# The last feed-forward layer's first batch: rows turned by VectorE and DMA in place of TensorE, their low parts by GpSimd

## The chip, the cores and the metric

The kernel runs on one core of a Trainium2 chip. The metric is the device time of one execution in microseconds (us); before the change the median of three runs is 2222.36 us (2220.96 to 2223.24). The engines are named as in the profile: PE is TensorE, DVE is VectorE, ACT is ScalarE, POOL is GpSimd, and SP is the engine whose queue issues most DMAs.

## The reference, cut to what matters

The input is a batch of 8 sequences of 512 rows and 512 columns, float32. Two layers follow each other, and each of their four parts ends in a layer norm over the rows:

```python
x = layernorm(x + attention0(x))        # 16 heads of 32, causal
x = layernorm(x + experts(x))           # 8 experts, the two best of each row
# layer 1's attention: 8 heads of 64 over 2 groups of keys, no mask
h = norm_scale * x / (rms(x) + EPS) * split_scale
out = softmax(q @ k.T / 8) @ v          # q, k, v are products of h
x = layernorm(x + out @ Wo.T)
# layer 1's feed-forward part, integer weights
g = silu(x @ ((wq_gate - 128) * s_gate).T)
u = x @ ((wq_up - 128) * s_up).T
x = layernorm((g * u) @ ((wq_down - 128) * s_down).T)
```

The change lies where the third part (layer 1's attention) ends and the fourth (the "last FFN") begins.

## The kernel before, in words

**The last FFN** (`IntegerFfn`) works on one batch of 512 rows after another. Its matmuls need the batch's rows turned: columns of `x` on the 128 partitions, rows along the free axis, as four tiles of 128 x 512. Each turned tile is kept as two: `x_high`, the value rounded to the format that TensorE multiplies fast (fp32r), and `x_low`, the rest, so that two fast products stand for one float32 product. ACT writes the high part and DVE subtracts it from the turned tile for the low part.

There are two ways to turn the rows. `split` (L1102 to L1110), used for batch 0 alone, has TensorE transpose sixteen blocks of 128 x 128, four to a PSUM tile (L1108); ACT copies the tile to `x_high` (L1109) and DVE takes `x_low` (L1110). `blocks` and `parts` (L1083 to L1099), used for batches 1 to 7 inside the FFN, have DVE transpose 32 x 32 blocks (L88, four instructions of 128 x 512), send the room to DRAM with four DMAs (L93) and fetch it with a fifth (L96), which puts the blocks where they belong; then ACT casts (L1098) and DVE subtracts (L1099) from SBUF. This way leaves the rows in another order along the free axis, and `hidden` (L1135) undoes it where it reads the products and writes their halves: for `b` above 0 the access patterns of L1148's tile and of the two halves (L1153, L1154) go through `Turn.by_tile`.

Batch 0 is turned while layer 1's attention does its last batch, number 7.

**Layer 1's attention** (`Attention1`) does a batch in eight rounds, 0 to 7. A batch has four queries, `g` = 0 to 3, of two heads each, and each query has four blocks of 128 keys, `kt` = 0 to 3. A round does two blocks of one query, so query `g` takes rounds 2g and 2g + 1. The order inside a round is written out by hand in `batches` and holds on PE, DVE, ACT and POOL; SP's DMAs are ordered by a scheduler. A round issues, in this order:

1. `score`: four matmuls into two PSUM tiles `sc` (L1702), and two exponentials of 128 x 1024 on ACT (L1705) into two of four buffers `p`;
2. `add` for the blocks of the round before: DVE sums the `p` tiles into `total` (L1713), one instruction in an odd round, two in an even one;
3. the pieces that `plan` lists for the round: a query's projection (L1607, eight matmul records, and ACT's copy L1609), the output projection of the batch before (L1670, then DVE's L1676, L1684, L1685);
4. `product` for the blocks of the round before: `av` (L1724);
5. where that completes a query, so in even rounds, `normalise` (L1729): two matmuls `rs` of `total` with ones (L1732), ACT's copy with a sum (`watch_sums`, L995), DVE's reciprocal (L1735) and product (L1742), and POOL's `watch_inverses` (L998), which adds the reciprocal to a running total.

So `rs` on PE waits for the DVE's sums of the query, and the exponentials of a round wait for buffers of `p` that `add` and `product` of two rounds before have to have read. `total`, `r_inv` and the query's tile `hT` have one buffer each.

In batch 7 `plan` puts query 1 in round 0, query 2 in round 1, query 3 in round 5, output projections in rounds 2, 3, 4 and 7, and `split` of one of the four tiles in each of rounds 0, 2, 4 and 6.

Of the kernel before, what the change touches and what calls it, by code (L numbers as in the profile page):

```python
# [9 lines left out]
F32 = mybir.dt.float32  # L10
# [4 lines left out]
ALU = mybir.AluOpType  # L15
# [3 lines left out]
P = 128  # L19
NB = 8  # L20
S = 512
D = 512
NT = S // P
ND = D // P
# [33 lines left out]
def in_order(tc, *engines):  # L58


    return tc.manual_schedule(engines={mybir.EngineType.PE, *engines})
# [11 lines left out]
class Turn:  # L73
# [11 lines left out]
    def blocks(self, room, t, x):  # L85

        out = room.rearrange("p (j t c) -> p j t c", t=self.n, c=32)[:, :, t, :]
        self.nc.vector.transpose(out, x.rearrange("p (j c) -> p j c", c=32))  # L88
# [328 lines left out]
class Router:  # L417
# [70 lines left out]
    def logits(self, x1T, ps):  # L488

        for c in range(ND):  # L490
            self.nc.tensor.matmul(ps[32 * c : 32 * (c + 1), :], lhsT=self.wr[:, c, :], rhs=x1T[:, c, :],
                                  start=True, stop=True)

    def choose(self, b, parts, ps):

        nc, small = self.nc, self.small
# [300 lines left out]
class Tiles:  # L797
# [83 lines left out]
    def weights(self, i, c):  # L881
        at = self.ats[i]
        if i < N_FIXED:
            return self.w[:, at + c * 512 : at + (c + 1) * 512]
        return self.w[:, bass.ds(at + c * 512, 512)]
# [180 lines left out]
class IntegerFfn:  # L1066
# [13 lines left out]
        self.halves[b] = [pool.tile([P, ND, S], F32R, tag=f"rows{i}", name=f"x3_{part}")  # L1080
                          for i, part in enumerate(("high", "low"))]

    def blocks(self, b, t):  # L1083

        if t == 0:
            self.room(b)
            self.turned = self.raw.tile([P, ND * S], F32, tag="turned", name="turned")
        turn = self.turns[b % 2]
        turn.blocks(self.turned, t, self.env.xs[b][:, t, :])
        if t == NT - 1:  # L1090
            turn.out(self.turned)
            turn.back(self.turned)

    def parts(self, b, c):

        high, low = (half[:, c, :] for half in self.halves[b])
        x = self.turned[:, ts(c, S)]
        self.nc.scalar.copy(high, x)  # L1098
        self.nc.vector.tensor_tensor(low, x, high.bitcast(F32), ALU.subtract)  # L1099

    def split(self, b, c, ps):

        nc = self.nc
        if c == 0:
            self.room(b)
        high, low = self.halves[b]
        for t in range(NT):
            nc.tensor.transpose(ps[:, ts(t, P)], self.env.xs[b][:, t, ts(c, P)], self.env.ident)  # L1108
        nc.scalar.copy(high[:, c, :], ps)  # L1109
        nc.vector.tensor_tensor(low[:, c, :], ps, high[:, c, :].bitcast(F32), ALU.subtract)  # L1110

    def run(self, held_out, last_norm):
        tc, nc, weights = self.env.tc, self.nc, self.weights
# [21 lines left out]
    def hidden(self, b, c, held):  # L1135

        nc, vec, work, weights = self.nc, self.env.vec, self.work, self.weights
        g = self.p_gu.tile([P, S], F32, tag="g", name="ps_g1")
        u = self.p_gu.tile([P, S], F32, tag="u", name="ps_u1")
        for ps, w in ((g, weights(2 * c)), (u, weights(2 * c + 1))):  # L1140
            for dc in range(ND):
                for i, x in enumerate(self.halves[b]):
                    nc.tensor.matmul(ps, lhsT=w[:, ts(dc, P)], rhs=x[:, dc, :],  # L1143
                                     start=(dc, i) == (0, 0), stop=(dc, i) == (ND - 1, 1))
        sg = work.tile([P, S], F32, tag="sg", name="sg1", bufs=2)
        nc.scalar.activation(sg, g, AF.Silu, scale=vec[:, V_SG + c : V_SG + c + 1])
        hT = work.tile([P, S], F32, tag="hT", name="hT2", bufs=2)
        nc.vector.scalar_tensor_tensor(hT, u, vec[:, V_SU + c : V_SU + c + 1], sg, ALU.mult, ALU.mult)  # L1148
        high, low = (self.late.tile([P, S], F32R, tag=f"h{i}", name="h_late") if held else
                     work.tile([P, S], F32R, tag=f"h{i}", name="h_half", bufs=2) for i in range(2))  # L1150

        hT, *halves = [self.turns[0].by_tile(a, back) if b else a for a, back in ((hT, True), (high, False), (low, False))]
        nc.scalar.copy(halves[0], hT)  # L1153
        nc.vector.tensor_tensor(halves[1], hT, halves[0].bitcast(F32), ALU.subtract)  # L1154
        return high, low
# [381 lines left out]
class Attention1:  # L1537
# [94 lines left out]
        for part in (self.w_qkv[:, c, :], self.w_qkv[:, ND : ND + 2, ts(c, P)]):  # L1632
            self.nc.scalar.mul(part, part, self.nss[:, c : c + 1])

    def run(self, weights, split):

        with ExitStack() as phase:
            self.work = work = phase.enter_context(self.env.tc.tile_pool(name="c_work", bufs=1, reuse_waits="tile"))
            p_sc = phase.enter_context(self.env.tc.tile_pool(name="c_sc", bufs=2, space=PSUM, reuse_waits="tile"))
            p_av = phase.enter_context(self.env.tc.tile_pool(name="c_av", bufs=2, space=PSUM, reuse_waits="tile"))  # L1640
            with in_order(self.env.tc, mybir.EngineType.DVE, mybir.EngineType.Activation, mybir.EngineType.Pool):
                return self.batches(work, p_sc, p_av, weights, split)

    def batches(self, work, p_sc, p_av, weights, split):
        env, nc, guard, state, HD = self.env, self.nc, self.guard, self.state, self.HD
        xs = env.xs
        scale = 1.0 / math.sqrt(HD)
# [14 lines left out]
        def project(b, t):  # L1662
            ps = self.mm([P, D], "ps_o1")
            project_groups(b, t, ps, range(ND))
            residual(b, t, ps)
            statistics(b, t)
# [24 lines left out]
        def norm(b):  # L1691
            st = state.pop(b)
            for t in range(NT):
                x = xs[b][:, t, :]
                nc.vector.tensor_scalar(x, x, st["mv"][:, t, 0:1], st["rstd"][:, t : t + 1], ALU.subtract, ALU.mult)
# [49 lines left out]
        def plan(b):  # L1745


            todo = [[] for _ in range(ND * NT // 2)]
            here = pieces.pop(b)
            first, final = b == 0, b == NB - 1  # L1750
            if first:
                pieces[1] = self.prepare(1)
                todo[0] += [lambda t=t: pieces[1]["fetch"](t) for t in range(NT)]
            then = pieces.get(b + 1)
            if b:
                for t, i in enumerate((2, 3, 4, 7) if final else (2, 3, 4, 5)):
                    todo[i].append(lambda t=t: project(b - 1, t))
                if not final:
                    todo[6].append(lambda: norm(b - 1))
            for g, i in zip((1, 2, 3), (1, 3, 5) if first else (0, 1, 5) if final else (0, 1, 3)):  # L1760
                todo[i].append(lambda g=g: here["query"](g))
            if final:
                for c, i in enumerate((0, 2, 4, 6)):
                    todo[i].append(lambda c=c: split(0, c, self.mm([P, S], "ps_xT")))
            else:
                if first:

                    for t, i in ((2, 1), (3, 2)):
                        todo[i].append(lambda t=t: then["sum"](t))
                        todo[i + 2].append(lambda t=t: then["stat"](t))  # L1770
                for t, i in ((0, 1), (1, 2)) if first else ((0, 0), (1, 1), (2, 1), (3, 2)):
                    todo[i].append(lambda t=t: then["add"](t))
                if first:
                    todo[4].append(then["deviations"])

                    todo[5].insert(0, then["norm"])
                    todo[6] += [lambda c=c: then["turn"](c) for c in range(ND)]
                else:
                    todo[2].append(then["deviations"])
                    todo[3].append(then["norm"])  # L1780
                    todo[3] += [lambda t=t: then["blocks"](t) for t in range(NT)]
                todo[6].append(then["key"])
                todo[7] += [then["value"], lambda: then["query"](0)]
                if b + 2 < NB:
                    after = pieces[b + 2] = self.prepare(b + 2)
                    todo[7] += [lambda t=t: after["fetch"](t) for t in range(NT)]
            for i in (7,) if first else (1, 7) if final else (5, 7):
                todo[i] += [weights.convert, lambda: weights.load(work, 2, weights.FIRST)]
            return todo

        last = []
        for b in range(NB):
            for i, thunks in enumerate(plan(b)):
                units = [(b, u // NT, u % NT) for u in (2 * i, 2 * i + 1)]
                ps = [score(*unit) for unit in units]
# [12 lines left out]
        b = NB - 1  # L1808
# [16 lines left out]
def usual_pass(tc, ins, held_out):  # L1825
    nc = tc.nc
    with ExitStack() as ctx:
# [4 lines left out]
        with tc.tile_pool(name="a_mm", bufs=2, space=PSUM) as p_mm, ExitStack() as attn1_ctx:  # L1832
            with tc.tile_pool(name="routes", bufs=1, side="right") as routes, \
# [11 lines left out]
                attention = Attention1(env, guard, router, rows, own, p_mm, dram)  # L1845
# [15 lines left out]
            weights = IntegerWeights(env, guard)  # L1861
            weights.open(ctx.enter_context(tc.tile_pool(name="c_weights", bufs=1, side="right")), weights.FIRST)
            ffn = IntegerFfn(env, guard, weights, rows, dram)
            last_norm = attention.run(weights, ffn.split)
        ffn.run(held_out, last_norm)


# [236 lines left out]
def _layout(a):  # L2104
# [18 lines left out]
    def hidden(w):  # L2123
        return w.reshape(NHID, P, ND, P).transpose(0, 3, 2, 1).reshape(NHID, P, D)

    gate_up_q = np.stack([hidden(a["L1_ffn_wq_gate"]), hidden(a["L1_ffn_wq_up"])], axis=1).reshape(2 * NHID, P, D)

    def rows(n):
# [43 lines left out]
```

## Time and profile before

| What | us |
|---|---|
| median of the runs | 2222.36 |
| the profiled execution | 2228.55 |
| its span, first to last instruction | 2226.8 |
| PE busy | 2191.9 (98%) |
| DVE busy | 1273.7 (57%) |
| ACT busy | 632.0 (28%) |
| POOL busy | 487.6 (22%) |
| batch 7's rounds in the span | 1643 to 1702 |
| first matmul of the last FFN | 1722.78 |

Times within an execution are counted from the span's start. The profiled execution is 6.2 us above the median of the runs. "Busy" counts instructions of an engine; an engine that is idle shows the wait and who released it.

### The profile page before, as it was taken

The page shows a single profiled execution, that of the slowest core. Times are in us where ns is not written, and L with a number is a line of the kernel's source. Part 1 is how long each engine was busy: PE and PEld are TensorE (multiplying, and loading weights), DVE is VectorE, ACT ScalarE, POOL GpSimd, SP SyncE. Part 2 cuts the span into 40 slices and gives each one's busy share as a digit, 9 for nine tenths or more (in the row PEclk, how much of TensorE's full clock was granted, in tenths as well). Part 3 has the DMA queues.
Part 4 walks back from the last instruction along what each step waited for, and adds up shares of the span by engine and source line. Part 5 has one row for each costly group of instructions (what it writes and reads, how often), then busy time and mean ns, then how long its engine had stood idle before and what let it go on. Part 6 is the DMA issues. An engine that isn't in the chain of part 4 may idle for free. (4 is left out here: it accounts for less than half of the span.)

```text
span 2226.8 us, 23678 instructions
## 1 busy us (share of the span) xinstructions
PE 2191.9 (98%) x9006; PEld 1116.6 (50%) x9006; DVE 1273.7 (57%) x2032; ACT 632.0 (28%) x917; POOL 487.6 (22%) x489
## 2 busy tenths in 40 slices
PE   9999999999999999999999999999999999999997
PEld 3344444444444444444443333333343778888876
DVE  3556666666666633323316887798757655555443
ACT  2332323323233232122124333223332222222222
POOL 2322423234132333122105222222211000000000
PEclk9999999999999899999999999999999999999999
DMA  8010101101022216888735212312110321111000
GB/s 297 20 57 1 57 10 48 58 1 58 5 71 94 85 57 181 227 218 214 191 114 193 80 57 86 95 55 77 45 32 13 109 78 57 57 57 57 20 20 21
DMA packets 146428, 182.20 MB, mean 82 GB/s; under 512 B 60530, under 2 KB 89202, under 8 KB 144514
## 3 DMA queue, kind: packets, MB, share of 16 engines
q1 hardware_dynamic: 135024, 144.91, 21.0%
q0 software_dynamic: 10560, 34.61, 5.5%
q8 instruction: 74, 1.21, 0.2%
q10 hardware_dynamic: 722, 1.07, 0.1%
q14 instruction: 48, 0.39, 0.1%
HBM read 117.38 MB, written 63.18 MB: 81 GB/s over the span
## 5 line engine op out<-in xcount | busy, mean ns | idle before, releaser
L903 PE MATMUL ps_gu<-experts,xrT 128*128 128x512 f32 (+1 forms) x520 | 248.8, 601 | 0.0
L1360 ACT ACTIVATE p<-sc 128x2048 f32<-128x2048 f32 (+1 forms) x96 | 152.8, 1592 | 190.0 <-PE sc L1356 183.1
L1148 DVE SCALAR_TENSOR_TENSOR hT<-ps_u,vec,sg 128x512 f32<-128x512 f32 x88 | 65.6, 745 | 195.2 <-PE ps_u L1143 195.2
L1365 POOL TENSOR_SCALAR_AFFINE_SELECT p<-p 128x512 f32<-128x512 f32 x128 | 91.6, 729 | 385.2 <-ACT p L1360 378.5
L1159 PE MATMUL ps_f<-ffn_w,h_half 128*128 128x512 f32 x672 | 170.2, 394 | 0.6 <-issue 0.4
L998 POOL TENSOR_TENSOR g_total<-g_total,r_inv 128x512 f32<-128x512 f32 x64 | 89.7, 1401 | 358.3 <-DVE r_inv L1735 283.0
L1705 ACT ACTIVATE p<-sc 128x1024 f32<-128x1024 f32 x128 | 124.0, 1021 | 105.9 <-PE sc L1702 100.8
L1735 DVE RECIPROCAL r_inv<-r_inv 128x512 f32<-128x512 f32 x32 | 107.1, 3346 | 78.8 <-ACT r_inv L995 78.8
L1388 DVE TENSOR_TENSOR p<-p 128x1536 f32<-128x1536 f32 (+2 forms) x96 | 129.4, 1348 | 39.2 <-POOL p L1365 22.2
L905 DVE TENSOR_TENSOR h<-ps_gu,h 128x256 f32<-128x256 f32 x67 | 28.4, 424 | 212.8 <-ACT h L904 212.8
L903 PEld LDWEIGHTS ps_gu<-experts,xrT 128*128 128x128 f32 x520 | 96.2, 197 | 89.7 <-issue 89.5
L1159 PEld LDWEIGHTS ps_f<-ffn_w,h_half 128*128 128x128 f32 x672 | 124.4, 188 | 33.0 <-DVE h_half L1154 5.6
L1143 PE MATMUL ps_g<-x_high,ffn_w 128*128 128x512 f32 x352 | 138.9, 395 | 0.8 <-DVE x L1676 0.8
L1143 PE MATMUL ps_g<-x_low,ffn_w 128*128 128x512 f32 x352 | 139.1, 395 | 0.0
L1143 PE MATMUL ps_u<-x_low,ffn_w 128*128 128x512 f32 x352 | 138.8, 394 | 0.0
L1143 PE MATMUL ps_u<-x_high,ffn_w 128*128 128x512 f32 x352 | 138.7, 394 | 0.0
L919 PE MATMUL ps_y<-experts,hT 128*128 128x512 f32 (+1 forms) x272 | 127.9, 593 | 0.5 <-ACT hT L913 0.5
L1702 PE MATMUL sc<-qT,kT 64*128 64x512 f32 x512 | 127.3, 615 | 1.0 <-ACT qT L1609 0.7
L1292 PE MATMUL ps_q<-experts 128*128 128x512 f32 x256 | 121.1, 615 | 4.4 <-DMA experts<-in_xT 4.4
L1724 PE MATMUL av<-p,v 128*64 128x512 f32 x512 | 123.8, 605 | 0.0
L1285 PE MATMUL ps_v<-experts 128*128 128x512 f32 x256 | 118.0, 609 | 3.3 <-DVE v L1287 3.3
L1670 PE MATMUL ps_o<-attn_out,aoT 128*128 128x512 f32 x256 | 117.9, 605 | 0.8 <-ACT r_inv L995 0.8
(262 smaller groups left out, 3438.5 us busy)
## 6 DMA issues: line engine op xcount, KB each, us to landing
results<-y SPq DMA_DIRECT2D x68, 256.0 KB, 2.3
turned<-turned SPq DMA_DIRECT2D x56, 256.0 KB, 4.1
pair<-xrT SPq DMA_DIRECT2D x25, 512.0 KB, 3.4
xrT<-pair SPq DMA_DIRECT2D x100, 128.0 KB, 4.5
x<-in_x SPq DMA_DIRECT2D x8, 1024.0 KB, 7.5
experts<-in_gate_up SPq DMA_DIRECT2D x8, 1024.0 KB, 10.8
rows<-x SPq DMA_DIRECT2D x32, 256.0 KB, 2.0
x<-rows SPq DMA_DIRECT2D x8, 1024.0 KB, 15.5
```

Source lines behind the costliest of these rows:

```text
L903: nc.tensor.matmul(ps, lhsT=xT[:, c, :], rhs=self.weights(i, c), start=c == 0, stop=c == ND - 1)
L919: self.nc.tensor.matmul(ps, lhsT=hT[:, c, :], rhs=self.weights(i, ND + c), start=c == 0, stop=c == self.NI - 1)
L1143: nc.tensor.matmul(ps, lhsT=w[:, ts(dc, P)], rhs=x[:, dc, :], start=(dc, i) == (0, 0), stop=(dc, i) == (ND - 1, 1))
L1159: self.nc.tensor.matmul(os[t], lhsT=h[:, ts(t, P)], rhs=self.weights(2 * NHID + c), start=(c, i) == (0, 0), stop=(c, i) == (NHID - 1, 1))
L1285: nc.tensor.matmul(ps, lhsT=xts[b][:, c, ts(t, P)], rhs=wv[:, c, :], start=c == 0, stop=c == ND - 1)
L1292: nc.tensor.matmul(ps, lhsT=wq[:, g, ts(c, P)], rhs=xts[b][:, c, :], start=c == 0, stop=c == ND - 1)
L1360: nc.scalar.activation(p, sc[:, :, :width], AF.Exp, scale=scale)
L1388: nc.vector.tensor_tensor(total[:, :, P * kt :], total[:, :, P * kt :], p[:, :, at : at + w], ALU.add)
L1670: nc.tensor.matmul(ps, lhsT=state[b]["aoT"][:, c, ts(t, P)], rhs=w_out[:, c, :], start=c == 0, stop=c == ND - 1)
L1702: nc.tensor.matmul(sc[:, j, :], lhsT=st["kT"][hs, ts(kt, P)], rhs=st["qT"][g][hs, :], start=True, stop=True)
L1705: nc.scalar.activation(p, sc, AF.Exp, scale=scale)
L1724: nc.tensor.matmul(st["av"][HD * j : HD * (j + 1), :], lhsT=st["v"][:, kt, HD * j : HD * (j + 1)], rhs=p[:, j, :], start=kt == 0, stop=kt ...
```

## The change

Batch 0's rows are turned the way that the others are. `split` is gone. Its pieces in rounds 0, 2, 4 and 6 give way to `blocks` for all four tiles in round 3 and `parts` for two tiles each in rounds 5 and 6. `blocks` gets a room: the buffer of the attention's own turned rows `hT`, which is free once batch 7's last query has been projected; so that query moves from round 5 to round 3, ahead of `blocks`. In `parts` the subtraction of batch 0 goes to GpSimd, that of the other batches stays on VectorE. `hidden` now undoes the order of the rows for every batch. The calls that convert and load weights move from rounds 1 and 7 to rounds 0 and 1; the twenty units that they serve are loaded and converted by batch 5, so in batch 7 they do nothing, before and after.

```diff
-    def blocks(self, b, t):
+    def blocks(self, b, t, room=None):
         if t == 0:
             self.room(b)
-            self.turned = self.raw.tile([P, ND * S], F32, tag="turned", name="turned")
+            self.turned = self.raw.tile([P, ND * S], F32, tag="turned", name="turned") if room is None else room
...
         self.nc.scalar.copy(high, x)
-        self.nc.vector.tensor_tensor(low, x, high.bitcast(F32), ALU.subtract)
-
-    def split(self, b, c, ps):
...
+        engine = self.nc.vector if b else self.nc.gpsimd
+        engine.tensor_tensor(low, x, high.bitcast(F32), ALU.subtract)
...
-        hT, *halves = [self.turns[0].by_tile(a, back) if b else a for a, back in ((hT, True), (high, False), (low, False))]
+        hT, *halves = [self.turns[0].by_tile(a, back) for a, back in ((hT, True), (high, False), (low, False))]
...
-            for g, i in zip((1, 2, 3), (1, 3, 5) if first else (0, 1, 5) if final else (0, 1, 3)):
+            for g, i in zip((1, 2, 3), (1, 3, 5) if first else (0, 1, 3)):
                 todo[i].append(lambda g=g: here["query"](g))
             if final:
-                for c, i in enumerate((0, 2, 4, 6)):
-                    todo[i].append(lambda c=c: split(0, c, self.mm([P, S], "ps_xT")))
+                room = []
+                def blocks(t):
+                    if t == 0:
+                        room.append(self.own.tile([P, ND, S], F32, tag="hT", name="turned2"))
+                    ffn.blocks(0, t, room[0].rearrange("p k s -> p (k s)"))
+                todo[3] += [lambda t=t: blocks(t) for t in range(NT)]
+                for c, i in enumerate((5, 5, 6, 6)):
+                    todo[i].append(lambda c=c: ffn.parts(0, c))
...
-            for i in (7,) if first else (1, 7) if final else (5, 7):
+            for i in (7,) if first else (0, 1) if final else (5, 7):
                 todo[i] += [weights.convert, lambda: weights.load(work, 2, weights.FIRST)]
```

More of the change, by code (lines that the diff above doesn't have):

```diff
@@ L1098, in parts @@
         self.nc.scalar.copy(high, x)
-        self.nc.vector.tensor_tensor(low, x, high.bitcast(F32), ALU.subtract)
-    def split(self, b, c, ps):
[L1103 to L1110, printed above, removed]
+        engine = self.nc.vector if b else self.nc.gpsimd
+        engine.tensor_tensor(low, x, high.bitcast(F32), ALU.subtract)
     def run(self, held_out, last_norm):
@@ L1633, in scale, with run @@
             self.nc.scalar.mul(part, part, self.nss[:, c : c + 1])
-    def run(self, weights, split):
+    def run(self, weights, ffn):
         with ExitStack() as phase:
@@ L1641, in run, with batches @@
             with in_order(self.env.tc, mybir.EngineType.DVE, mybir.EngineType.Activation, mybir.EngineType.Pool):
-                return self.batches(work, p_sc, p_av, weights, split)
-    def batches(self, work, p_sc, p_av, weights, split):
+                return self.batches(work, p_sc, p_av, weights, ffn)
+    def batches(self, work, p_sc, p_av, weights, ffn):
         env, nc, guard, state, HD = self.env, self.nc, self.guard, self.state, self.HD
@@ L1863, in usual_pass @@
             ffn = IntegerFfn(env, guard, weights, rows, dram)
-            last_norm = attention.run(weights, ffn.split)
+            last_norm = attention.run(weights, ffn)
         ffn.run(held_out, last_norm)
```

## The prediction

> **What bounds the kernel now.** I read the page first: PE is busy for 98% of the span at full clock, so a piece taken from PE is worth what it held of PE, and any new wait of PE costs its length.
>
> ```profile
> PE 2191.9 (98%) x9006; PEld 1116.6 (50%) x9006; DVE 1273.7 (57%) x2032; ACT 632.0 (28%) x917; POOL 487.6 (22%) x489
> PEclk9999999999999899999999999999999999999999
> ```
>
> Then PE's timeline from the `rs` of query 1 (round 4) to that of query 2 (round 6): no gap, and each row begins where the one before stops delivering. Starts are what to subtract.
>
> ```profile
> 1680.79 0.60 PE L1108 MATMUL ps_xT<-ident,x 128*128 128x128 f32 x4
> 1681.32 1.94 PE L1724 MATMUL av<-p,v 128*64 128x512 f32 x8
> 1683.09 1.03 PE L1732 MATMUL rs<-total,ones 128*64 128x512 f32 x4
> 1684.04 1.99 PE L1702 MATMUL sc<-qT,kT 64*128 64x512 f32 x8
> 1685.96 3.70 PE L1607 MATMUL ps_q<-hT,attn_qkv 128*128 128x512 f32 x8
> 1689.59 1.94 PE L1724 MATMUL av<-p,v 128*64 128x512 f32 x8
> 1691.46 1.99 PE L1702 MATMUL sc<-qT,kT 64*128 64x512 f32 x8
> 1693.38 0.66 PE L1108 MATMUL ps_xT<-ident,x 128*128 128x128 f32 x4
> 1693.96 1.94 PE L1724 MATMUL av<-p,v 128*64 128x512 f32 x8
> 1695.73 1.03 PE L1732 MATMUL rs<-total,ones 128*64 128x512 f32 x4
> ```
>
> DVE's and POOL's timelines in the same stretch show the chain that the second `rs` needs: reciprocal, product, three sums.
>
> ```profile
> 1684.94 3.35 DVE L1735 RECIPROCAL r_inv<-r_inv 128x512 f32<-128x512 f32 x1 [1.68 <-ACT r_inv L995]
> 1688.40 0.69 DVE L1742 TENSOR_TENSOR aoT<-av,r_inv 128x512 f32<-128x512 f32 x1
> 1689.00 1.71 DVE L1713 TENSOR_TENSOR total<-p,p 128x1024 f32<-128x1024 f32 x1
> 1690.82 2.56 DVE L1713 TENSOR_TENSOR total<-total,p 128x1024 f32<-128x1024 f32 x2
> 1688.37 1.26 POOL L998 TENSOR_TENSOR g_total<-g_total,r_inv 128x512 f32<-128x512 f32 x1 [14.86 <-DVE r_inv L1735]
> ```
>
> I call 1683.09 R. The sums end at R + 10.3, PE has other work until R + 12.64, so before the change the chain is covered by 2.3 us. The first sum takes 1.71 us; the same instruction alone takes 1.22 (its shortest, in the rows of L1713). It starts at 1689.00 and POOL's addition ends at 1689.63: two DVE inputs in SBUF wait for a POOL instruction that reads SBUF. Elsewhere the same, both ways: at 247.63 a POOL addition that began under a DVE sum took 1.58 in place of 1.27.
>
> Last, windows around a wait of PE, for the clock (the column before the last two). PE idled 1.71 us until 278.97; the clock was half from 279.5 to 283.0.
>
> ```profile
> 278.97 5.40 PE L1285 MATMUL ps_v<-experts 128*128 128x512 f32 x8 [1.71 <-DVE v L1287]
> 279.00:283.00 4.00, 4.00 (x6) 1.69 (x7) 0.52 (x1) 0.25 (x1) 1.22 (x2) 0.57 0.00 0
> 283.00:286.00 3.00, 3.00 (x9) 1.33 (x8) 0.69 (x1) 0.00 (x0) 0.00 (x0) 1.00 0.00 0
> ```
>
> **The change part by part.**
>
> *PE loses sixteen transposes.* By the starts they hold PE for 0.52, 0.53, 0.53 and 0.58 us: 2.16 us, a saving in full.
>
> *Query 3 moves from round 5 to round 3.* Its 3.63 us of PE stay, but they leave the stretch above, and its transposes (0.58) go too. Between the two `rs` PE then has 0.95 (`rs`) + 1.92 (scores) + 1.87 (`av`) + 1.92 (scores) + 1.77 (`av`) = 8.43 us. The DVE chain starts with the same `rs` and is no shorter: R + 10.3, with 0.1 to the next engine R + 10.4. Cover of 2.3 us becomes a wait of PE of 1.95 us, even if nothing else slows the chain. In round 3 the query is followed by `av`, scores, projection and `av` before an `rs`, 9.2 us, so no chain gets tight there. Its ACT copy (0.58) moves with it into a round with 3 us to spare.
>
> *DVE gains four transposes and loses four subtractions.* 2.48 us for four L88 rows (1608.86 in batch 6) against 4 x 0.67. The transposes sit behind the projection's statistics in round 3 and wait for PE to finish query 3, at about R - 9.0, to end at R - 6.5. Behind them queue the two sums of round 4 (2.5 us, R - 4.0), needed by the `rs` at R: 4 us to spare, cost nothing. If PE were late there, the sums would be as late as PE, no more.
>
> *Five DMAs on SP.* Four out, one back. In batch 6 the transposes ended at 1611.34, the four went out from 1611.37, the fifth was issued at 1618.90, and one like it lands in 4.7 to 6.5 us: 12.3 to 14.1 us from transposes to rows, R + 5.8 to R + 7.6. In SP's order after the change nothing stands between the fifth DMA and the FFN's weight loads, which ran at 1722 before: those are not held up.
>
> *ACT.* The four casts go from PSUM (0.59) to SBUF (0.62). Round 5's two stand behind its exponentials, which end at R + 4.1, and in front of round 6's. They wait for the rows until R + 5.8 and are done at R + 7.1. Round 6's first exponential needs the `p` buffers that the first sum frees at R + 7.6, so this wait is covered by 0.5 us; landing at the late end it costs the exponentials 1.3 us, and those feed nothing on PE before the `rs`.
>
> *POOL gains four subtractions*, queued between the `watch_inverses` of rounds 4 and 6. Price of one: 1.27 (L998 alone), up to 1.42 (L794's two at 235.35, beside DVE work); POOL writing fp32r is in no row, so I keep as ends half of that and 2.5, twice L998. The first can start when its cast is done, R + 6.6, finds the first sum running, and goes at R + 7.6; the second sum, due at R + 7.7, then finds it running. Alternating, as DVE's and POOL's rows did at 235: POOL to 9.0, DVE to 10.2, POOL to 11.5, DVE to 12.7 (1.35 and 1.2 each). PE's wait becomes 12.8 - 8.43 = 4.3 us. The last two subtractions come after round 6's casts and meet only the reciprocal, one input. Ends: 1.95 us (no meeting) and 6.7 us (2.5 for each of two).
>
> *The clock.* A PE wait of 0.84 us at 1710 left the clock full; 1.71 us gave 3.5 us of half clock, so 1.75 us lost, and 1.77 us at 721 gave 6.7 us, so 3.35 lost, before matmuls that fill only a quarter of the array. Here the work beside the wait has 64 of 128 rows or columns. I take 2.3, between the two and nearer the first, ends 0 and 3.35.
>
> The Trainium skill ("TensorE: Matmul & The Clock Gate", the section on HAM oscillation) puts the limit at idle gaps of more than about 3.4 us. The rows disagree, since 1.71 us sufficed; by the page a wait of 1.95 us would keep the clock and the sum for it would be -0.1 us, while a wait of 4.3 us pays either way. The skill's "SBUF — State Buffer" (who interferes with whom) says that the second of such a pair of DVE and GpSimd instructions is blocked until the first has finished, which speaks against low parts on GpSimd here; by it the second and third sum wait as in my row-based order.
>
> *`hidden` for batch 0.* DVE's L1154 takes 0.64 at its shortest and 0.69 in the turned batches, ACT's L1153 0.61 against 0.62. Eleven chunks, DVE 0.6 us in all, beside matmuls: in the FFN's first 60 us PE idles 1.3 us in total. I take 0.05, ends -0.1 and 0.6.
>
> **Sum:** -2.16 + 4.3 + 2.3 + 0.05 = +4.5 us. The profiled execution (2228.55) would become 2233.0; applied to the median of the runs, 2222.36, it gives 2226.9, +0.20%. 0.2% is 4.4 us, about what a measurement of this kernel can tell from no change: the sum lies on that edge.
>
> **The rivals.**
>
> *Not slower: the chain doesn't hold PE.* In round 6 the low parts don't meet the sums (the rows land late, so that only one or none comes before R + 10) and the clock stays. Then -2.16 + 1.95 = -0.2, 2222.1; with one meeting +1.1. It decides from the point where wait and clock together cost less than 2.16 us. For it: the rows may land 1.5 us later than I have them. Against it: the 1.95 is there in any case, and a 1.71 us wait lost the clock.
>
> *The plain gain.* Nothing waits: -2.16, 2220.2. It would need the DVE chain to be 2 us shorter than all its rows show (3.35, 0.69, 1.71, 2.56). To be faster by over 0.2% something unseen has to add 2.3 us.
>
> *GpSimd is the bound.* It is slow at fp32r: at 2.5 us each the wait is 6.7, with 3.35 of clock: +7.9, 2230.3. Nothing shows it, nothing excludes it.
>
> *The rows land late and hold ACT.* It decides from a landing at about R + 8.5, 15 us after the transposes; beyond that each us delays the exponentials and then the next `watch_sums`. DMA is idle in this stretch (share 0.00), so batch 6's 12.3 us is the likely one. Price at 2 us later: +1, on top of a chain without a collision.
>
> **How the numbers follow.** Wait with collision and lost clock 0.62 (spread about +2.2 to +6.5, more than half of it above +4.4); GpSimd slow 0.13; chain alone or one meeting with the clock kept, or late rows, 0.17; plain gain 0.08. Slower by over 0.2%: 0.54; within: 0.40; faster: 0.06, mostly for what I don't see. Range 2221.6 to 2230.0: it leaves out the plain gain and the worst of the slow GpSimd.
>
> **What would show it.** After: no ps_xT; between the `rs` of queries 1 and 2 an idle PE of 3 to 5 us, released by DVE `total` L1713; POOL subtractions of about 1.3 us between the sums of L1713, of which two rise from 1.2 to over 2; PEclk at half for 3 to 7 us behind it; the FFN's batch 0 unchanged. Wrong, if PE idles under 2 us there, if the clock holds, or if POOL's rows are far from 1.3.

## The result and the profile after

The changed kernel takes 2227.14 us (median of 13 runs, 2224.21 to 2230.32), the kernel before 2223.24 us (13 runs beside it). The ratio is 1.0017 with a 95% interval of 1.0009 to 1.0024: slower by 3.8 us. The forecast was 2226.9 us, +0.20%. One execution of the kernel e5 below took 2290.46 us at a mean granted clock of 0.945, a slower state of the chip; it is left out of its ratio and of the counts of runs.

The profiled execution spans 2228.6 us against 2226.8, only 1.8 us more, and this difference alone would mislead. Batch 7's first scores start at 1640.20 us in this trace and at 1643.08 in the one before: 2.9 us were won before the changed code is reached, in layer 0; the wait and the half clock at 279 us that the prediction shows, for one, are missing in this execution. What the change does is seen in the **stage** from the first scores of batch 7 to the first matmul of the last FFN: 1643.08 to 1722.78 before, 79.70 us; 1640.20 to 1724.23 after, 84.03 us. From there to the end it is 504.0 us before and 504.4 after. All comparisons of traces below use this stage. Its ends before, with the `rs` of query 3 between them, and its ends after:

```profile
1643.08 1.99 PE L1702 MATMUL sc<-qT,kT 64*128 64x512 f32 x8
1708.59 1.08 PE L1732 MATMUL rs<-total,ones 128*64 128x512 f32 x4
1722.78 0.50 PE L1143 MATMUL ps_g<-x_high,ffn_w 128*128 128x512 f32 x1 [0.84 <-DVE x L1676]
1640.20 1.99 PE L1693 MATMUL sc<-qT,kT 64*128 64x512 f32 x8
1724.23 0.50 PE L1134 MATMUL ps_g<-x_high,ffn_w 128*128 128x512 f32 x1 [0.84 <-DVE x L1667]
```

The lines of `kernel.py` behind `parts` are lower by up to nine in the changed kernel: L1704 is the sum that was L1713, L1723 is `rs`, L1101 the subtraction.

PE's share, from the page, is what it was:

```profile
PE 2191.2 (98%) x8990; PEld 1114.0 (50%) x8990; DVE 1275.9 (57%) x2032; ACT 632.3 (28%) x917; POOL 495.2 (22%) x493
```

PE's timeline of the changed kernel from the `rs` of query 1 to that of query 3 answers to the ten lines shown of before (start, length, engine, line, operation; in brackets the idle time ahead and who ended it):

```profile
1682.33 1.03 PE L1723 MATMUL rs<-total,ones 128*64 128x512 f32 x4
1683.28 1.99 PE L1693 MATMUL sc<-qT,kT 64*128 64x512 f32 x8
1685.20 1.94 PE L1715 MATMUL av<-p,v 128*64 128x512 f32 x8
1687.07 1.99 PE L1693 MATMUL sc<-qT,kT 64*128 64x512 f32 x8
1688.99 1.94 PE L1715 MATMUL av<-p,v 128*64 128x512 f32 x8
1694.44 1.98 PE L1723 MATMUL rs<-total,ones 128*64 128x512 f32 x4 [3.52 <-DVE total L1704]
1696.35 3.79 PE L1693 MATMUL sc<-qT,kT 64*128 64x512 f32 x8
1700.07 3.70 PE L1661 MATMUL ps_o<-attn_out,aoT 128*128 128x512 f32 x8
...
1710.05 1.08 PE L1723 MATMUL rs<-total,ones 128*64 128x512 f32 x4
```

The transposes and the query are gone, and PE idles for 3.52 us until DVE's `total`. From `rs` to `rs` it takes 12.11 us for 8.43 us of work: a wait of 3.68 us by the starts. Behind the wait the same matmuls take twice as long: `rs` 1.98 in place of 1.03, the scores 3.79 in place of 1.99. To the next `rs` it is 15.61 us where it was 12.86 (1708.59 - 1695.73).

DVE's and POOL's timelines show why `total` is late; the single POOL instructions come from narrow windows.

```profile
1684.18 3.35 DVE L1726 RECIPROCAL r_inv<-r_inv 128x512 f32<-128x512 f32 x1 [1.82 <-ACT r_inv L995]
1687.64 0.69 DVE L1733 TENSOR_TENSOR aoT<-av,r_inv 128x512 f32<-128x512 f32 x1
1688.24 1.72 DVE L1704 TENSOR_TENSOR total<-p,p 128x1024 f32<-128x1024 f32 x1
1690.07 2.11 DVE L1704 TENSOR_TENSOR total<-total,p 128x1024 f32<-128x1024 f32 x1
1692.29 2.10 DVE L1704 TENSOR_TENSOR total<-total,p 128x1024 f32<-128x1024 f32 x1
1689.35 1.75 POOL L1101 TENSOR_TENSOR x_low<-turned,x_high 128x512 fp32r<-128x512 f32 x1 [0.47 <-ACT x_high L1098]
1691.06 2.25 POOL L1101 TENSOR_TENSOR x_low<-turned,x_high 128x512 fp32r<-128x512 f32 x1
1693.27 2.24 POOL L1101 TENSOR_TENSOR x_low<-turned,x_high 128x512 fp32r<-128x512 f32 x1
1695.48 1.26 POOL L1101 TENSOR_TENSOR x_low<-turned,x_high 128x512 fp32r<-128x512 f32 x1
```

The two engines take turns. A sum that takes 1.22 us alone takes 2.11 and 2.10, and a subtraction that takes 1.26 alone, the fourth, takes 2.25 and 2.24 while sums run. Before, the two sums took 2.56 us together, here 4.32.

The clock, from windows over the stretch (PE's busy time first; the column before the last two is the granted clock):

```profile
1691.00:1693.00 2.00, 0.00 (x0) 0.00 (x0) 1.90 (x2) 2.00 (x4) 2.00 (x2) 1.00 0.00 0
1694.00:1700.00 6.00, 5.55 (x12) 1.48 (x12) 3.14 (x2) 1.71 (x3) 2.73 (x2) 0.50 0.00 0
1701.00:1703.00 2.00, 2.00 (x6) 0.95 (x5) 2.00 (x2) 0.20 (x1) 0.95 (x1) 1.00 0.00 0
```

In windows of 0.1 us the clock is still 1.00 up to 1693.20, 0.73 in the next window and 0.50 from 1693.30; it is full again at 1700.1. So the half clock lasts some 6.8 us and begins inside the wait, 2.3 us after PE went idle (1694.44 - 3.52 = 1690.92) and 1.2 us before its next matmul; some 5.6 us of it fall on matmuls, which at half clock costs about 2.8 us.

So the stage's +4.33 us are -2.16 (transposes) + 3.68 (wait) + 2.75 (half clock from the second `rs` to the third, 15.61 - 12.86), and 0.06 unexplained.

### The profile page after: what moved, and what is told of

The parts are those of the page before. It is cut to its first block, busy times and chain, and to the rows that moved or that the text cites. A ratio compares the mean times of both kernels' runs of the same rounds, so it can differ in the third digit from the quotient of the medians.

```text
span 2228.6 us, 23664 instructions
## 1 busy us (share of the span) xinstructions
PE 2191.2 (98%) x8990; PEld 1114.0 (50%) x8990; DVE 1275.9 (57%) x2032; ACT 632.3 (28%) x917; POOL 495.2 (22%) x493
```

## The experiments

Ratios are to the kernel before, timed in the same session. The waits and stages are from one profiled execution of each kernel.

| Kernel | wait of `rs`, us | stage, us | median, us | before, us | ratio, 95% |
|---|---|---|---|---|---|
| before | 0 | 79.70 | | | |
| changed | 3.52 | 84.03 | 2227.14 | 2223.24 | 1.0017 (1.0009 to 1.0024) |
| e1 projection to round 6 | 0 | 77.60 | 2221.40 | 2224.50 | 0.9990 (0.9979 to 1.0000) |
| e2 subtractions later | 1.76 | 79.58 | 2223.86 | 2224.50 | 1.0004 (0.9995 to 1.0012) |
| e3 query alone | 1.17 | 80.89 | 2225.48 | 2224.50 | 1.0010 (1.0002 to 1.0019) |
| e4 subtractions on DVE | 2.69 | 80.52 | 2225.55 | 2224.50 | 1.0011 (1.0002 to 1.0021) |
| e5 filled wait | 0 | 81.35 | 2224.14 | 2223.85 | 1.0004 (0.9996 to 1.0013) |
| e6 changed, again | 3.52 | 81.35 | 2227.01 | 2223.85 | 1.0015 (1.0007 to 1.0024) |
| e7 as e4, again | 2.70 | 80.52 | 2225.75 | 2223.85 | 1.0012 (1.0004 to 1.0021) |
| e8 as e1, again | 0 | 77.61 | 2221.44 | 2223.62 | 0.9991 (0.9982 to 1.0001) |
| e9 e1 and e2 together | 0 | 77.60 | 2221.68 | 2223.62 | 0.9989 (0.9980 to 0.9998) |

**e1: give PE work in the stretch.** Against the changed kernel:

```diff
-                for t, i in enumerate((2, 3, 4, 7) if final else (2, 3, 4, 5)):
+                for t, i in enumerate((2, 3, 6, 7) if final else (2, 3, 4, 5)):
```

> The changed kernel with the output projection of row tile 2 in round 6 (behind the sums) in place of round 4, so that PE has 3.62 us more work between the rs of queries 1 and 2: 12.05 us in place of 8.43. Theory (PE waits for the DVE chain that GpSimd stretches, and loses clock behind that wait): the chain ends at R + 12.1, the wait falls from 3.5 to 0.3 us or less, the clock stays full, the stage from round 0's scores to the FFN's first matmul falls from 84 to about 77.6 us, against 79.7 in the kernel before; time 2.1 us below the kernel before, about 2221. Rival (the way over DRAM costs by itself: casts that hold ACT, rows that come late, the other order of the rows in the FFN): the stage stays above 79.7 us and the time above the kernel before.

The stage is the theory's 77.60 us, but the chain isn't the one that was expected: it ends at R + 10.3 (R being the first `rs`) and not at R + 12.1, because POOL's subtractions and the sums don't meet here. With a projection less in round 4 the first `rs` comes 3.6 us earlier against the rows, the subtractions start at 1684.13, and the sums, from 1681.46, took their 2.55 us. So e1 covers an unstretched chain; the stretched one is covered in e5. PE's timeline of e1, with no bracket at the second `rs`:

```profile
1673.72 1.03 PE L1723 MATMUL rs<-total,ones 128*64 128x512 f32 x4
...
1680.38 3.70 PE L1661 MATMUL ps_o<-attn_out,aoT 128*128 128x512 f32 x8
1684.01 1.94 PE L1715 MATMUL av<-p,v 128*64 128x512 f32 x8
1685.78 1.03 PE L1723 MATMUL rs<-total,ones 128*64 128x512 f32 x4
```

The way over DRAM, the casts, the other order of the rows and GpSimd are all still in this kernel, and it has the whole saving of the transposes: 79.70 - 77.60 = 2.10 us. The rival falls.

**e2: subtractions behind the sums.** Against the changed kernel:

```diff
-                for c, i in enumerate((5, 5, 6, 6)):
+                for c, i in enumerate((6, 6, 7, 7)):
```

> The changed kernel with the casts and subtractions of the four tiles in rounds 6, 6, 7, 7 in place of 5, 5, 6, 6, so that GpSimd's subtractions come behind the sums that the rs of query 2 needs. Theory: the sums take 1.2 us each again and the chain ends at R + 10.4, so PE waits 1.95 us; 84 - 1.7 = 82.3 us for the stage if the clock still falls for 6.7 us, 81.2 if for 3.5 us, 79.5 if it holds. Rival (the meeting of GpSimd and VectorE is not what stretches the wait): wait 3.5 us, stage 84.

DVE's sums and POOL's subtractions of e2 no longer meet, and PE waits 1.76 us:

```profile
1686.87 2.56 DVE L1704 TENSOR_TENSOR total<-total,p 128x1024 f32<-128x1024 f32 x2
1689.40 2.50 POOL L1101 TENSOR_TENSOR x_low<-turned,x_high 128x512 fp32r<-128x512 f32 x2 [3.72 <-ACT x_high L1098]
1689.47 1.08 PE L1723 MATMUL rs<-total,ones 128*64 128x512 f32 x4 [1.76 <-DVE total L1704]
```

Half of the wait is GpSimd's: 3.52 against 1.76. The edit also moves ACT's casts, but they aren't what stretches the sums: e4 below keeps them at their early places, and its sums take 2.47 us. The other half of the wait is the chain itself. The clock held here, so the stage is about that of the prediction's first rival (-0.2): 79.58 against 79.70.

**e3: only the query moved.** Against the kernel before:

```diff
-            for g, i in zip((1, 2, 3), (1, 3, 5) if first else (0, 1, 5) if final else (0, 1, 3)):
+            for g, i in zip((1, 2, 3), (1, 3, 5) if first else (0, 1, 3)):
```

> The kernel before, with only the last query moved from round 5 to round 3; rows still turned by TensorE. Theory (taking the query out of the stretch is what uncovers the DVE chain): PE has 9.0 us there and the chain 10.4, so PE waits 1.4 us although nothing else is changed; stage 79.7 + 1.4 = 81.1 us with full clock, 82.8 to 84.4 if the clock falls. Rival (GpSimd's subtractions alone make the wait): no wait, stage 79.7, time as before.

```profile
1690.12 1.08 PE L1732 MATMUL rs<-total,ones 128*64 128x512 f32 x4 [1.17 <-DVE total L1713]
```

A wait of 1.17 us appears with TensorE's transposes still there and no subtraction on GpSimd, and the stage is longer by 1.19 us. Making room for the turned rows costs by itself, before a row is turned.

**e4: the subtractions on VectorE.** Against the changed kernel:

```diff
-        engine = self.nc.vector if b else self.nc.gpsimd
+        engine = self.nc.vector
```

> The changed kernel with batch 0's subtractions on VectorE again, at the same places. Theory (what counts is that they stand ahead of the sums, on whichever engine): two of them, 1.35 us, go between the first sum and the other two, the chain ends at R + 11.8, PE waits 3.3 us in place of 3.5, the clock falls the same, stage 83.7. Rival (the shared access of GpSimd and VectorE is the cause and VectorE alone is free of it): wait 1.95 us or less, stage 82.3 or less.

```profile
1687.78 1.28 DVE L1101 TENSOR_TENSOR x_low<-turned,x_high 128x512 fp32r<-128x512 f32 x2
1688.99 2.47 DVE L1704 TENSOR_TENSOR total<-total,p 128x1024 f32<-128x1024 f32 x2
1691.51 1.08 PE L1723 MATMUL rs<-total,ones 128*64 128x512 f32 x4 [2.69 <-DVE total L1704]
```

Neither side was right in full. The wait fell to 2.69 us, less than the 3.3 of the theory and more than the rival's 1.95: DVE passes two subtractions in 1.28 us, 0.93 us of it added to a wait of 1.76. And the clock held, where I had it fall. So on VectorE the two subtractions cost less than where GpSimd does them beside it (0.93 against 1.76 us), and neither is free.

**e5: useless work in the wait.** Against the changed kernel; the added projection's result is read by nothing:

```diff
                 for c, i in enumerate((5, 5, 6, 6)):
                     todo[i].append(lambda c=c: ffn.parts(0, c))
+                todo[6].append(lambda: project_groups(b - 1, 3, self.mm([P, D], "ps_fill"), range(ND)))
```

> The changed kernel with useless work on PE in the wait: in round 6 the output projection of row tile 3 is computed once more into a PSUM tile that nothing reads, 3.62 us of full matmuls between the scores and the av. Theory (3.5 us of the stage's loss are the wait, another 2.75 the half clock behind it): the rs of query 2 starts where it did, about 12.1 us after the one before, PE is not idle, the clock stays full, the next rs follows in 12.86 us in place of 15.61; stage 81.3 us, time 2.7 us below the changed kernel although more is computed. Rival (the half clock comes from the stretch of matmuls that fill half of the array, or from chance, and not from the idle PE): the half clock comes in spite of the filling, stage 84 or longer.

PE's timeline of e5:

```profile
1685.83 3.70 PE L1661 MATMUL ps_fill<-attn_out,aoT 128*128 128x512 f32 x8
1689.46 1.94 PE L1715 MATMUL av<-p,v 128*64 128x512 f32 x8
1691.30 1.08 PE L1723 MATMUL rs<-total,ones 128*64 128x512 f32 x4
```

The stage is 81.35 us with full clock, as expected, and DVE's two sums are as long as in the changed kernel (4.32 us from 1686.92): the added work takes the place of the wait. By the medians of one session the kernel that computes more takes 2224.14 us and the changed kernel 2227.01: 2.9 us less. The two intervals (1.0004 and 1.0015) overlap a little; the means of the 11 runs each (without that of 2290.46 us) differ by 2.6 us, with 0.9 to 4.2 us as a resampled 95% interval. The 2.75 us that were expected hold only for executions that lose the clock, and e6 shows that not all do.

**e6 and e7: the clock once more.**

> The changed kernel once more, timed beside the others on one chip. If the loss of clock behind a wait of 3.5 us is a rule and no accident of one execution: wait 3.5 us, half clock for 3.4 to 6.7 us again, stage 82.5 to 84, ratio to the kernel before about 1.0017. If it was an accident: full clock in this profile, stage 81.3, ratio about 1.0007.

> The changed kernel with batch 0's subtractions on VectorE, a second execution: its wait of 2.7 us kept the full clock in the first. If there is a limit between 2.7 and 3.5 us in this stage: full clock again, stage 80.5, about 1 us above the kernel before. If it is where the wait falls in time that decides: half clock in this one, stage 82 to 84.

In e6's profile the wait is the same 3.52 us and the clock stays full:

```profile
1693.31 1.08 PE L1723 MATMUL rs<-total,ones 128*64 128x512 f32 x4 [3.52 <-DVE total L1704]
1694.00:1700.00 6.00, 6.00 (x20) 2.26 (x20) 4.68 (x3) 2.63 (x4) 2.88 (x3) 1.00 0.00 0
```

So a wait of this length doesn't always lose the clock; it comes in some executions. The time shows both kinds: a kernel that always kept the clock would be at +1.65 us (81.35 - 79.70), one that always lost it at +4.33, and the ratios of 1.0017 and 1.0015 say +3.8 and +3.3. e7 repeated e4: 2.70 us, full clock in the profile. The mean granted clock that comes with each run points the same way: 0.993 or lower in 11 of 24 runs of the changed kernel, 6 of 23 with the wait of 2.7 us, none of 24 with shorter waits (e2, e3), 3 of 85 runs of the kernel before, and 1 of 45 of those without any wait (e1, e5, e8, e9). The mean covers layer 0's clock as well, and the limit of 0.993 was chosen afterwards. In the first session the seven such runs were slower than the other six (2229.0 against 2225.9 us in the mean); among e6's runs the four were not (2227.1 against 2227.4). So the counts support a loss in a part of the executions, about half by them and 0.6 to 0.8 by the times, and don't prove it for this place.

**e8 and e9: a version that beats both.**

> The kernel with row tile 2's output projection in round 6, once more, for a firmer ratio: stage 77.6 us, no wait of PE for the sums of query 2, ratio to the kernel before 0.9990 (2.1 us of transposes saved) and, with the first time's runs, an interval that lies below 1. If its first result was luck: ratio 1.000 or above.

> Row tile 2's output projection in round 6 and the casts and subtractions in rounds 6, 6, 7, 7, so that GpSimd meets no sum and PE waits for none. Theory: the wait was gone already, so freeing VectorE of GpSimd buys nothing more, stage 77.6 us, ratio 0.9990. Rival (GpSimd beside VectorE costs the stage something by itself): stage and ratio below those of the kernel with the projection alone moved.

The stage is 77.61 and 77.60 us. Three results, 0.9990, 0.9991 and 0.9989, agree on 2.2 us below the kernel before; e9's interval, 0.9980 to 0.9998, lies below 1, the other two reach it. That e9 gains nothing over e1 and e8 says little of GpSimd beside VectorE, since their subtractions meet the sums hardly at all (in e8 they start at 1687.57, and the sums end at 1687.73). In e5 the sums are stretched, and PE, with enough to do, doesn't wait for them.

## Why the prediction was right

- *Transposes, -2.16.* Right: 2.10 in e1, where nothing covers it.
- *The query's move uncovers the DVE chain, 1.95 us of wait.* Right: 1.76 us listed in e2, 1.92 by the starts (1689.47 - 1679.12 - 8.43), and 1.17 in e3, where 0.58 us of transposes remain.
- *GpSimd's subtractions ahead of the sums raise the wait to 4.3 us.* The mechanism is in the trace, turn by turn; the size was too large by 0.6: 3.68. I had each meeting cost the sum a whole subtraction, 1.2 to 1.35 us. Each cost 0.9: a pair of a sum and a subtraction takes 2.2 us from start to start (1690.07 to 1692.29 on DVE), less than the 1.22 + 1.26 that they take alone.
- *GpSimd slow at writing fp32r.* The rival falls: 1.26 us, as for plain float32.
- *Rows in time.* The casts started at 1688.65 in the first profile, R + 6.3, inside the forecast R + 5.8 to R + 7.6. Round 6's exponentials were released by the first sum and not by the casts, as worked out:

```profile
1688.65 1.14 ACT L1098 CAST x_high<-turned 128x512 fp32r<-128x512 f32 x2 [2.25 <-DMA turned<-turned]
1690.08 1.94 ACT L1696 ACTIVATE p<-sc 128x1024 f32<-128x1024 f32 x2 [0.29 <-DVE total L1704]
```

- *The clock, 2.3 us.* This is the term that came out by luck as much as by reading. I took it for a fixed price; it is 2.75 us in one profile of the changed kernel and nothing in the other, and a held clock was among my signs of being wrong. The measured ratio less the +1.65 of the stage with full clock leaves 1.7 to 2.1 us as its mean, and the interval of each ratio is 1.6 to 2 us to either side. So of the sum's parts the wait was 0.6 us too long and the clock, as far as that tells, 0.2 to 0.6 too dear, and the sum, +4.5, lies 0.7 to 1.2 us above the measured +3.3 to +3.8, inside the range.
- *The limit for the clock.* The Trainium skill's limit of about 3.4 us idle ("TensorE: Matmul & The Clock Gate", on HAM oscillation) sorts this stage's profiles better than the rows I set against it: waits of 1.17, 1.76, 2.69 and 2.70 us kept the clock, one of two waits of 3.52 lost it. But no such limit is shown: where the 3.52 us lost it, the clock fell after 2.3 us of idle, 6 of 23 runs with 2.7 us have a low mean clock, and the prediction's rows of 1.71 and 1.77 us lost it too. Those two stood among matmuls of 32 rows or columns; whether that made the difference no run here tells. (By the page's limit the prediction's sum for a wait of 1.95 us is -0.16 and not -0.1.)
- *`hidden` in the other order.* From the FFN's first matmul to the end 504.0 us before, 504.1 in e1 and in e2, 504.4 in the changed kernel: a few tenths at most, inside the ends of -0.1 and 0.6, and too little to tell from nothing.

## What to carry to other kernels

Before a piece of work is moved off a busy engine's stretch, add up what is left of it there and set it beside the other engines' chain that runs from the stretch's first instruction to its last; the piece may be the cover. Here 2.1 us of transposes were saved and 3.7 us of wait bought with them, and moving another piece into the gap turned the loss into the gain that was there all along. Work given to GpSimd isn't free for VectorE while both read two tensors from SBUF.

## What the runs showed of the hardware that was not expected

The same wait of PE, 3.52 us at the same place of the same program, came with some 6.8 us of half clock in one execution, from 2.3 us into the wait on, and with none in another, so that a single profile prices it at 2.75 us or at zero; several runs are needed, and the stage's time with full clock has to be kept apart. And a wait filled with 3.62 us of useless matmuls made the kernel faster by 2.9 us in the median.
